# Branch hints, split first experts and three reordered places in a four-layer model with two mixtures of experts

## The chip, the cores and the metric

The kernel runs on one core of one Trainium2 chip. It is one launch that computes a whole model of four layers. The metric is the device time of one execution in microseconds (us). Before the change it is 2608.06 us, the median of three runs (2607.92 to 2608.73).

## The reference

The input `x` has 32 sequences of 64 tokens with 512 features: 2048 tokens, which the kernel takes as 16 tiles of 128. Each layer adds a residual. What is computed, cut to what matters (all in float32, and the weights are inputs):

```python
x = x + ffn0(einsum('bct,bcd->bdt', x, W0[subject]))   # attention, then shared expert
                                                       # + 7 experts, top 2 of sigmoid
x = x + ffn1(einsum('bct,bcd->bdt', x, W1[subject]))   # 32 experts, top 4, softmax gates
x = x + ffn2(x @ W.T + lora(x, adapter))               # soft mixture of 16 experts
x = x + ffn3(paged_attention(x, cache, tables, lens))  # linear layer on int8 values

# ffn1, for one token t and its 4 chosen experts:
gate = min(t @ w_gate[e] + b_gate[e], 7);  up = clip(t @ w_up[e] + b_up[e], -7, 7)
y += softmax(top4)[k] * (((up + 1) * gate * sigmoid(1.702 * gate)) @ w_down[e] + b_down[e])

# ffn2, with x_ln the layer norm of a token (gamma, beta) and x_n its l2 norm:
logits = x_n @ mu_n                                    # 16 experts x 128 slots
slots  = x_ln.T @ softmax(logits, over experts)
out    = softmax(logits, over all slots) @ (gelu(slots @ W1 + b1) @ W2 + b2)
```

`ffn0` and `ffn1` are sparse: a token goes to two or four experts only.

## The kernel before, in words

`program` (L2700) runs four functions, one for each layer; each hands its loads for the next one on, so that work of the next layer fills gaps of this one. Engines are called by name: PE is the tensor engine, DVE the vector engine, ACT the scalar engine, POOL GpSimd, SP the queue that issues most DMAs. Each engine executes its own instructions in order. A scheduler places the instructions of the program on the engines; what goes through `pin` (L314), or through an engine taken from `held`, stays in the order in which the program issues it, and `follow` in `Moe.run` chains the matmuls of the expert stage in order.

**The sparse layers.** Class `Moe` (L844; `Ranked`, L1285, for layer 1) gives each expert room for a fixed number of rows: 7 times 640 in layer 0 (35 tiles of rows), and 256 to 352 for each of 32 experts in layer 1 (71 tiles). A routing stage decides for each token its experts and its slot in them. `Moe.run` (L1142) then walks over *units*: an expert of 640 rows is two units of 320 (`UNIT`), a smaller one is one unit (L886 to L892). `turn` (L1166) transposes a gathered tile of 128 rows, in whose columns are the rows of one or more units (`of_unit`); in layer 0 DVE multiplies them by the norm's weights on the way out of PSUM (L1177), in layer 1 ACT and DVE copy in turn. `into` (L1181) does the first two matrix products of a unit, each half of 128 hidden columns in two groups of eight 128x128 matmuls `gu`, and the activation (`l0_expert`, `l1_expert`). `out_of` (L1197) multiplies one tile of rows with the last matrix, adds the bias in layer 1 and stores the tile to `ys`. Transposes of the next unit's tiles and finished tiles are woven between the groups of a unit. `rows_to` issues the gathers on POOL, `weights` and `bias_of` issue loads on SP, and `rank` is a generator that, in layer 1, sorts the experts by their load while the first unit is under way. Before the loop, all tiles of unit 0 are gathered and turned.

After the last tile, `beyond` (L1037) counts the token-expert pairs that found no room: it sums them on DVE (`more`, L1041), converts them (`number`, L1043), loads the number into a register of each engine and, under `tc.If(n > 0)` (L1048), runs a slow body for them. With these inputs the number is 0, and each engine jumps over the body. The body has several hundred instructions on DVE (some 450 in layer 0 and 880 in layer 1), and on POOL 49 and 283.

**The routing of layer 1.** `Mixed.run` (L1575) goes in steps `s` over the 16 token tiles: mix with the subject's matrix (`mix`), transpose (`turn`), logits (`route`, `logits`), pick (`choose`). From step 11 on the logits come straight as `rp` in `route`. At the steps of `GROUPS`, a generator `Ranked.put` is started for 4 or 2 tiles: alternately DVE and PE, it forms one-hot rows, counts (`at`), places and a `table` of tokens, and `go(engine)` advances those that wait for that engine. The last lines empty the generators, and `Ranked.end` (L1360) turns the table into the first experts' token lists (`tokens`, `fixedp`, `fixed`) that the first gathers wait for. The gates' softmax stands behind it in `layer1` (L1660 to L1668).

**Layer 2.** `layer2` (L1729) first sums the experts' rows for tiles 0 and 1 (`combined`, L1256: a gather `yk` by POOL and a multiply-add on DVE, L1264, four times a tile), runs `Lora` (L1878: transposes L1888, adapter product `ap` L1897, `am` on DVE L1901, product `yp` L1909 and L1910) for both tiles and the norm (`l2_norm_pieces`, L1925) of tile 0, whose multiplies with gamma and beta lie on POOL (L1937, L1938). `transpose4` (L366, matmuls at L371) turns the normed tile. Then each step `i` makes the two softmaxes of tile `i` (`Softmaxes`) and mixes tile `i-1` (`Mix`): `turn` (`ep`), `dispatch` (`hp`, `h`), `combine` (`gp`, `gT`) and `project` (`out`). Step 1 has an order of its own, written out under `early`. There `over_slots` (L2014) makes a matmul `bp` in PSUM and four subtractions and exponentials from it (`lT`, L2020), and `Mix.total` (L2080) makes the matmul `dp` (L2083) and its reciprocal `rd` (L2085). `ep`, `bp` and `dp` use the same two PSUM buffers (tag `tp`) in turn.

## Time and profile before

| | us |
|---|---|
| median of the runs | 2608.06 |
| the profiled execution | 2563.57 |
| its span | 2561.5 |
| PE busy in the span | 2442.1 |
| DVE, POOL and ACT busy | 1405.8, 905.8 and 718.3 |
| mean clock granted to PE, share of full speed | 0.974 |

The stages by time in the profiled execution, with PE's busy time and the granted clock in each:

| stretch, us | what runs there | PE busy, us | clock |
|---|---|---|---|
| 340 to 376 | end of layer 0's attention | 29.0 of 36 | 0.76 |
| 376 to 384 | start of layer 0's experts | 2.8 of 8 | 0.79 |
| 640 to 700 | end of layer 1's routing | 48.0 of 60 | 0.76 |
| 700 to 1120 | layer 1's experts | 412 of 420 | 0.98 |
| 1120 to 1160 | end of layer 1, start of layer 2 | 17.2 of 40 | 0.73 |
| 1160 to 2145 | layer 2 | 977.6 of 985 | 0.99 |
| 2290 to 2562 | layer 3's last part | 261 of 272 | |

All times and rows come from one execution, taken by the hardware profiler. A row of the timeline gives the start, the length, the engine, the line in the kernel, the operation with its output and inputs and their shapes, and in brackets how long the engine was idle before, and what ended that. `x4` is a run of like instructions. DVEq, SPq or POOLq is the part of an engine that issues. PEclk in the page is the granted clock in 40 equal slices of the span, in tenths. The profiled execution is shorter than the median of the runs by 44.5 us; differences are read against it, and its rows are not those of the median run.

### The profile page before, as it was taken

What the parts mean: (1) busy time and instruction counts of PE and PEld (TensorE: products, weight loads), DVE (VectorE), ACT (ScalarE), POOL (GpSimd) and SP (SyncE); (2) the same over time, 40 slices, a digit from 0 to 9 for tenths busy, and PEclk for the clock granted to TensorE, in tenths of its full rate; (3) what the DMA queues carried; (4) which work ended last, traced back from release to release, by engine and by line L of the source; (5) the groups of instructions that cost most, each with busy time, mean ns of one, the idle gap of its engine ahead of it and who ended that gap; (6) DMA issues with size and microseconds to landing.
All of it is one profiled execution on the core that took longest, in us unless ns stands there. A gap on an engine that the chain in (4) does not pass through costs nothing.

```text
span 2561.5 us, 42341 instructions
## 1 busy us (share of the span) xinstructions
PE 2442.1 (95%) x16533; PEld 1612.1 (63%) x16533; DVE 1405.8 (55%) x3456; ACT 718.3 (28%) x1508; POOL 905.8 (35%) x961
## 2 busy tenths in 40 slices
PE   6999989999799999979999999999999999979998
PEld 4776766666566666747666666666666665445554
DVE  3666756834745554436544544444545432657886
ACT  2444521112211111102222222222222221246664
POOL 2223325615144444523333333333333322564440
PEclk9999989999799999989999999999999999989999
DMA  2234325536456976834222222222222314424441
GB/s 102 93 138 153 128 75 199 169 120 225 161 194 229 373 275 233 296 123 150 69 73 75 74 73 73 73 76 76 74 76 76 97 57 144 165 58 134 140 140 38
DMA packets 132566, 339.35 MB, mean 132 GB/s; under 512 B 23993, under 2 KB 25049, under 8 KB 125056
## 3 DMA queue, kind: packets, MB, share of 16 engines
q1 hardware_dynamic: 90720, 188.84, 21.4%
q0 software_dynamic: 41056, 141.89, 17.6%
q10 hardware_dynamic: 576, 5.77, 0.6%
q8 instruction: 134, 2.20, 0.4%
q14 instruction: 80, 0.66, 0.1%
HBM read 245.23 MB, written 107.22 MB: 138 GB/s over the span
## 4 chain that ended last, share of the span: by engine, by line
PE 50%; DVE 3%; POOL 1%; issue 1%; DMA 1%; ACT 0%; POOLq 0%; ACTq 0%; DVEq 0%; SPq 0%
PE out L2107 9%; PE lp L1964 9%; PE zp L2041 7%; PE pp L2421 3%; PE hp L2073 3%; PE gp L2096 3%; PE y L2669 2%; PE yp L1909 2%; PE op L2647 2%; PE pT L2622 2%; PE sp L2600 2%; PE ep L2050 1%; PE kp L2573 1%; PE ap L1897 1%; PE csum L2060 1%
## 5 line engine op out<-in xcount | busy, mean ns | idle before, releaser
L1190 PE MATMUL gu<-xT,wt 128*128 128x320 f32 (+3 forms) x1472 | 396.2, 416 | 1.0 <-DVE xT L1177 0.5
L1190 PEld LDWEIGHTS gu<-xT,wt 128*128 128x128 f32 x1472 | 276.0, 191 | 120.4 <-issue 51.2
L1964 PEld LDWEIGHTS lp<-xnT,sb_mu 128*128 128x128 f32 x2048 | 236.2, 194 | 9.1 <-issue 6.7
L1964 PE MATMUL lp<-xnT,sb_mu 128*128 128x128 f32 x2048 | 239.1, 277 | 1.8 <-DVE xnT L332 1.2
L2107 PE MATMUL out<-sb_w,gT 128*128 128x512 f32 x512 | 234.2, 600 | 0.0
L2041 PE MATMUL zp<-sb_w,xnT 128*128 128x512 f32 x512 | 226.5, 592 | 0.0
L1202 PE MATMUL y<-wt,hT 128*128 128x512 f32 (+2 forms) x544 | 199.9, 595 | 1.4 <-DVE yo L1210 0.9
L360 POOL DMA_INDIRECT kvst<-kv,gidx x96 | 96.4, 1004 | 286.9 <-DMA oldkv<-kvst 205.0
L2100 DVE COPY gT<-gp 128x512 f32<-128x512 f32 x64 | 44.3, 692 | 237.9 <-PE gp L2096 237.5
L2041 PEld LDWEIGHTS zp<-sb_w,xnT 128*128 128x128 f32 x512 | 93.7, 190 | 104.8 <-issue 102.5
L2107 PEld LDWEIGHTS out<-sb_w,gT 128*128 128x128 f32 x512 | 93.6, 191 | 103.9 <-issue 95.6
L360 POOL DMA_INDIRECT kvt<-newkv,oidx x96 | 100.3, 1045 | 128.4 <-DMA kvt<-oldkv 59.2
L360 POOL DMA_INDIRECT yk<-ys,slot x96 | 97.7, 1017 | 117.1 <-DVE pre L1291 74.9
L2078 ACT ACTIVATE h<-hp 128x512 f32<-128x512 f32 x128 | 69.5, 594 | 210.5 <-PE hp L2073 210.4
L1202 PEld LDWEIGHTS y<-wt,hT 128*128 128x128 f32 (+2 forms) x544 | 72.8, 166 | 63.8 <-issue 49.1
L360 POOL DMA_INDIRECT xr<-rows,stok x101 | 97.9, 969 | 42.2 <-issue 18.5
L840 POOL TENSOR_TENSOR ga<-ga,sg 128x288 f32<-128x288 f32 (+3 forms) x64 | 50.4, 788 | 166.9 <-ACT sg L836 166.7
L2118 POOL TENSOR_TENSOR xt<-xt,bc_bias 128x512 f32<-128x512 f32 x16 | 20.6, 1288 | 211.0 <-DMA x<-xt 196.3
L2096 PEld LDWEIGHTS gp<-lT,h 128*64 128x64 f32 x2048 | 65.8, 139 | 38.8 <-issue 26.5
L2611 ACT ACTIVATE s<-s,m 128x336 f32<-128x336 f32 x128 | 72.8, 570 | 57.3 <-DVE m L2607 56.1
L1969 DVE TENSOR_TENSOR lT<-lp,cmu 128x512 f32<-128x512 f32 x64 | 43.5, 680 | 80.2 <-PE lp L1964 80.2
L2052 ACT COPY ew<-ep 128x512 f32<-128x512 f32 x64 | 37.6, 589 | 177.0 <-PE ep L2050 177.0
(456 smaller groups left out, 4641.3 us busy)
## 6 DMA issues: line engine op xcount, KB each, us to landing
ys<-yo SPq DMA_DIRECT2D x106, 256.0 KB, 3.8
oldkv<-kvst SPq DMA_DIRECT2D x96, 224.0 KB, 2.2
kvt<-oldkv SPq DMA_DIRECT2D x96, 224.0 KB, 3.3
ys<-zero SPq DMA_DIRECT2D x10, 2048.0 KB, 8.0
xt<-x SPq DMA_DIRECT2D x62, 256.0 KB, 6.0
x<-xt SPq DMA_DIRECT2D x48, 256.0 KB, 2.0
wt<-w_e SPq DMA_DIRECT2D x7, 1536.0 KB, 6.7
sb_w<-w SPq DMA_DIRECT2D x5, 1024.0 KB, 14.7
```

The lines of the kernel that those rows point to most:

```text
L360: ins = self.nc.gpsimd.indirect_dma_start(out=out, out_offset=None, in_=src, in_offset=bass.IndirectOffsetOnAxis(ap=idx, axis=0), **kw)
L1190: follow(nc.tensor.matmul(o, wj[:, c, ic * P : (ic + 1) * P], xTs[u][:, c, 0:n], start=c == 0, stop=c == 3))
L1202: follow(nc.tensor.matmul(y[row : row + n, :], hTs[e][:, ic, col : col + n], wd[:, ic, :], start=ic == 0, stop=ic == 1,))
L1909: g.first(c, nc.tensor.matmul(yp, self.xT[:, c, :], w["w_2"][:, c, :], start=c == 0, stop=False))
L1964: g.first(e + c, nc.tensor.matmul(lp[:, e, :], w["mu"][:, c, (4 * q + e) * P : (4 * q + e + 1) * P], self.xnT[:, c, :], start=c == 0, stop ...
L2041: g.first(c, nc.tensor.matmul(zp, self.xnT[:, c, :], w["w1"][:, c, cols], start=c == 0, stop=c == 3))
L2073: g.first(e + b, nc.tensor.matmul(hp[:, b, e, :], self.ews[q][r, e, :], self.z[q][r, e * P : (e + 1) * P], start=True, stop=True))
L2078: g.pin(nc.scalar.activation(self.hs[q][b], hp[:, b], AF.Gelu))
L2096: g.first(e + b + k, nc.tensor.matmul(gp[r, e, cols], self.hs[q][b][:, e, r], self.lT[q][:, e, cols], start=True, stop=True))
L2107: g.first(e, nc.tensor.matmul(self.out, self.gTs[q][:, e, :], w["w2"][:, 4 * q + e, :], start=q + e == 0, stop=q + e == 6 and q == 3))
L2421: nc.tensor.matmul(pp, xT[i][:, c, :], (w["w_kv3"] if z else wq)[:, c, :], start=c == 0, stop=c == 3)
L2611: nc.scalar.activation(p, p, AF.Exp, bias=m, scale=-1.0, accum_out=tot)
```

## The change

It does five things. The first parts of the diff are a helper and its call: `hint` puts one instruction on PE, DVE, ACT and POOL that names the branch `beyond{E}` as likely taken, three row tiles ahead of the end of `Moe.run`; the branch gets a label. The first expert's first 320 rows, in both layers, become two units of 128 and 192 rows, and the steps of the unit loop at which gathers, loads and the ranking are issued move accordingly (in layer 1 the ranking advances at three named places and not at every group). In the routing, from step 11 on the youngest generator's PE part is issued ahead of the logits and the transpose; at the end the generators are emptied in a fixed order, and the gates' softmax, now a generator in `Ranked`, is cut in two: subtraction and exponential before the last table matmuls, sum, reciprocal and product behind `end`. In layer 2, tile 0's norm is taken in pieces between the parts of tile 1's `Lora`, its gamma and beta products go to DVE, and in step 1 `total` comes ahead of `over_slots`.

```diff
--- before.py
+++ after.py
@@ -31,6 +31,7 @@
 E1, K1, V1 = 32, 4, 56
 UNIT = 320
 WB = 4
+FIRST = 128
 
 
 RANK1 = [0, 1, 3, 4, 2, 6, 5] + list(range(7, 32))
@@ -310,6 +311,17 @@
                 )
 
         return step
+
+    def hint(self, label):
+
+        traced = self.nc.cur_bb.bb.instructions
+        before = len(traced)
+        kinds = mybir.EngineType
+        self.tc.mark_branch_hint_location(
+            label, "LikelyTaken", (kinds.PE, kinds.DVE, kinds.Activation, kinds.Pool)
+        )
+        for ins in list(traced)[before:]:
+            self.pin(SimpleNamespace(ins=ins))
 
     def pin(self, ins):
 
@@ -827,12 +839,12 @@
     nc.vector.tensor_tensor(hT, up, sg, ALU.mult)
 
 
-def l1_expert(g, sb, hT, gate, up, bias):
+def l1_expert(g, sb, hT, gate, up, bias, **kw):
 
     nc = g.nc
     ga = sb.tile([P, gate.shape[1]], F32, name="ga")
     nc.vector.tensor_scalar(ga, gate, bias[:, 0:1], 7.0, ALU.add, ALU.min)
-    sg = sb.tile([P, gate.shape[1]], F32, name="sg", **(dict(bufs=2) if gate.shape[1] > P else {}))
+    sg = sb.tile([P, gate.shape[1]], F32, name="sg", **kw)
     nc.scalar.activation(sg, ga, AF.Sigmoid, scale=1.702)
     up_ = sb.tile([P, gate.shape[1]], F32, name="up")
     nc.vector.tensor_scalar(up_, up, bias[:, 1:2], 7.0, ALU.add, ALU.min)
@@ -876,7 +888,8 @@
         self.units = []
         for e, cap in enumerate(caps):
             n = cap if cap < 2 * UNIT else UNIT
-            self.units += [(e, at, n) for at in range(0, cap, n)]
+            sizes = ([] if e else [FIRST, n - FIRST]) + [n] * (cap // n - (not e))
+            self.units += [(e, sum(sizes[:k]), size) for k, size in enumerate(sizes)]
         self.ends = [sum(n for _, _, n in self.units[: u + 1]) for u in range(len(self.units))]
         self.of_unit, self.of_expert = [[] for _ in range(self.tiles)], [[] for _ in range(self.tiles)]
         for parts, sizes, whole in (
@@ -1045,7 +1058,7 @@
             number[0:1, 0:1], min_val=0, max_val=N * K,
             skip_runtime_bounds_check_because="the number of pairs is at most N * K",
         )
-        with tc.If(n > 0), ExitStack() as ctx:
+        with tc.If(n > 0, label=f"beyond{E}"), ExitStack() as ctx:
             sb = ctx.enter_context(tc.tile_pool(name=f"vs{E}", bufs=1))
             ps = ctx.enter_context(tc.tile_pool(name=f"vps{E}", bufs=2, space=PSUM))
             iota = g.c("iota")
@@ -1143,7 +1156,6 @@
 
         g, nc, tc, E, K = self.g, self.g.nc, self.g.tc, self.E, self.K
         ends, most = self.ends, max(n for _, _, n in self.units)
-        single = len(self.units) == E
         last_of = {}
         for t, parts in enumerate(self.of_expert):
             for e, *_ in parts:
@@ -1182,7 +1194,7 @@
                 e, at, n = self.units[u]
                 wg, wu, _, bias = self.parts(self.weights(e))
                 if e not in hTs:
-                    hTs[e] = sb.tile([P, 2, max(self.caps)], F32, name="hT", bufs=3 if single else 2)
+                    hTs[e] = sb.tile([P, 2, max(self.caps)], F32, name="hT", bufs=3 if self.ranked else 2)
                 gu = []
                 for wj in (wg, wu):
                     o = ps.tile([P, most], F32, name="gu", tag="gu", bufs=4)[:, 0:n]
@@ -1192,9 +1204,12 @@
                         ))
                     gu.append(o)
                     yield
-                self.act(g, sb, hTs[e][:, ic, at : at + n], *gu, None if bias is None else bias[:, ic::2])
+                kw = dict(bias=None) if bias is None else dict(bias=bias[:, ic::2], bufs=2)
+                self.act(g, sb, hTs[e][:, ic, at : at + n], *gu, **kw)
 
             def out_of(t):
+                if t == self.tiles - 3:
+                    g.hint(f"beyond{E}")
                 y = ps.tile([P, D], F32, name="y", tag="y")
                 for ic in range(2):
                     for e, col, row, n in self.pieces[t]:
@@ -1226,26 +1241,27 @@
             for u in range(len(self.units)):
                 k = 0
                 e = self.units[u][0]
-                if not (self.ranked and u == 0):
-                    self.rows_to(tiles_to(u + 2))
+                if not (self.ranked and u < 2):
+                    self.rows_to(tiles_to(max(u, 1) + 2))
                 self.bias_of(e)
-                if 1 <= u < WB - 1:
-                    self.weights(u + 1 + self.ranked, not self.ranked)
+                if 2 <= u < WB:
+                    self.weights(u + self.ranked, not self.ranked)
                 for ic in range(2):
                     for _ in into(u, ic):
                         if turned < tiles_to(u + 1):
                             turn(turned)
                             turned += 1
                         k += 1
-                        next(ranking, None)
+                        if (u, k) in ((0, 3), (1, 1), (1, 2)):
+                            next(ranking, None)
                         if k > 1 and u and (done + 1) * P <= ends[u - 1]:
                             out_of(done)
                             done += 1
                             for old in range(E):
                                 if last_of[old] == done - 1 - self.ranked:
                                     self.weights(old + WB)
-                    if self.ranked and u == 0 and ic == 0:
-                        self.rows_to(tiles_to(2))
+                    if self.ranked and u == 1 and ic == 0:
+                        self.rows_to(tiles_to(3))
                         self.weights(FIXED1)
             while done < self.tiles:
                 out_of(done)
@@ -1357,6 +1373,18 @@
                     stop=i + j == NT - 1 and k == K - 1,
                 )
 
+    def softmax(self):
+
+        nc, gates, vals = self.g.held, self.gates, self.vals
+        shape = [P, NT, K1]
+        nc.vector.tensor_tensor(gates, vals[:, :, 0:K1], vals[:, :, 0:1].to_broadcast(shape), ALU.subtract)
+        nc.scalar.activation(gates, gates, AF.Exp)
+        yield
+        tot = self.keep.tile([P, NT], F32, name="tot1")
+        nc.vector.tensor_reduce(tot, gates, AX.X, ALU.add)
+        nc.vector.reciprocal(tot, tot)
+        nc.vector.tensor_tensor(gates, gates, tot.unsqueeze(2).to_broadcast(shape), ALU.mult)
+
     def end(self, ps):
 
         g, nc, tok, ident = self.g, self.g.held, self.tok, self.g.ident
@@ -1592,8 +1620,8 @@
                     self.late.append(late)
             del pieces[:n]
 
-        def go(engine):
-            for put in list(puts):
+        def go(engine, among=None):
+            for put in list(puts if among is None else among):
                 if put[1] == engine:
                     put[1] = next(put[0], None)
                     if put[1] is None:
@@ -1608,6 +1636,8 @@
             bridge.rest(self.wp, todo[0] + 2 + s)
             if s < NT:
                 self.mix(s)
+            if s not in SPLIT:
+                go("tensor", puts[-1:])
             self.adds(s + 1)
             fill()
             if s:
@@ -1630,11 +1660,14 @@
                 go("vector")
             if s in (10, 12):
                 m.weights((s - 10) // 2)
-        while puts:
-            go("tensor")
-            go("vector")
-        assert not pieces
+        for engine in ("tensor", "vector", "vector"):
+            go(engine)
+        gates = m.softmax()
+        next(gates)
+        go("tensor")
+        assert not puts and not pieces
         m.end(self.ps)
+        next(gates, None)
 
 
 def layer1(g, bridge, combined, beside, w2):
@@ -1656,16 +1689,6 @@
         for k in ("first", "pool"):
             w2[k] = w2[k]()
         m.ready(ctx)
-
-        gates, vals = m.gates, m.vals
-        nc.vector.tensor_tensor(
-            gates, vals[:, :, 0:K1], vals[:, :, 0:1].to_broadcast([P, NT, K1]), ALU.subtract
-        )
-        nc.scalar.activation(gates, gates, AF.Exp)
-        tot = keep.tile([P, NT], F32, name="tot1")
-        nc.vector.tensor_reduce(tot, gates, AX.X, ALU.add)
-        nc.vector.reciprocal(tot, tot)
-        nc.vector.tensor_tensor(gates, gates, tot.unsqueeze(2).to_broadcast([P, NT, K1]), ALU.mult)
 
         def ahead(sb, ps, i):
             if i < NT and i % 4 == 3:
@@ -1740,14 +1763,20 @@
         x = [combined(sb, 0, 3), combined(sb, 1, 3)]
         for k in ("gamma", "beta"):
             w[k] = g.load_bcast(wp, k)
-        yp = [Lora(g, w, sb, s2, ps, x[i], i).run() for i in range(2)]
-        xn = l2_norm(g, w, sb, s2, yp[0])
+        norm = l2_norm_pieces(g, w, sb, s2, Lora(g, w, sb, s2, ps, x[0], 0).run(), nc.vector)
+        lora = Lora(g, w, sb, s2, ps, x[1], 1)
+        lora.turn()
+        next(norm)
+        next(norm)
+        lora.adapter()
+        xn = next(norm)
+        yp = lora.product()
         w["b1"] = g.load_bcast(wp, "b1", eng=nc.scalar, later=True)
         for k in ("w2", "b2"):
             w[k] = g.load(wp, k, nc.scalar, True)
         w["bias3"] = g.load_bcast(wp, "bias3", eng=nc.scalar, later=True)
         xnT, nn = g.transpose4(ps, s2, xn[0], "xnT2"), xn[1]
-        xn = l2_norm(g, w, sb, s2, yp[1])
+        xn = l2_norm(g, w, sb, s2, yp)
 
 
         last = None
@@ -1788,9 +1817,9 @@
                 mix.dispatch(0)
                 norm = l2_norm_pieces(g, w, sb, s2, lora.product())
                 next(norm)
+                mix.total()
                 soft.over_slots()
                 mix.turn(2)
-                mix.total()
                 mix.combine(0)
                 mix.dispatch(1)
             else:
@@ -1922,7 +1951,7 @@
     return out
 
 
-def l2_norm_pieces(g, w, sb, s2, yp):
+def l2_norm_pieces(g, w, sb, s2, yp, eng=None):
     nc = g.nc
     st = s2.tile([P, 6], F32, name="st")
     g.pin(nc.vector.bn_stats(st, yp))
@@ -1934,8 +1963,10 @@
     yield
     xl = sb.tile([P, D], F32, name="xl")
     g.pin(nc.vector.tensor_scalar(xl, yp, mv[:, 0:1], rs, ALU.subtract, ALU.mult))
-    nc.gpsimd.tensor_tensor(xl, xl, w["gamma"], ALU.mult)
-    nc.gpsimd.tensor_tensor(xl, xl, w["beta"], ALU.add)
+    for k, op in (("gamma", ALU.mult), ("beta", ALU.add)):
+        ins = (eng or nc.gpsimd).tensor_tensor(xl, xl, w[k], op)
+        if eng:
+            g.pin(ins)
     sq = sb.tile([P, D], F32, name="sq2", tag="mx")
     ss = s2.tile([P, 1], F32, name="ss2")
     nc.scalar.activation(sq, xl, AF.Square, accum_out=ss)
```

## Prediction

> **What bounds the kernel now.** The page's head first: engine shares, slices, granted clock.

> ```profile
> span 2561.5 us, 42341 instructions
> PE 2442.1 (95%) x16533; PEld 1612.1 (63%) x16533; DVE 1405.8 (55%) x3456; ACT 718.3 (28%) x1508; POOL 905.8 (35%) x961
> PE   6999989999799999979999999999999999979998
> PEclk9999989999799999989999999999999999989999
> ```

> TensorE (PE) is busy 95% of the span; only 119 us are idle. The slices drop at the start, near 690 us (slice 11) and near 1130 us (slice 18), and the clock drops with them. A mended stall so pays twice: its own length, and the half-clock matmuls after it. Second view: the waits of PE between 1100 and 1260 us (total, times, longest), which carry the largest holes.

> ```profile
> PE tp L1888 <- DVE xt L1264: 16.9, 1, 16.9
> PE tp L371 <- DVE xl L1947: 3.8, 1, 3.8
> PE dp L2083 <- DVE lT L2020: 3.0, 1, 3.0
> ```

> Third: the timeline across both overflow branches (L1048: `n` is 0 here, so the body is jumped over), first the end of layer 1, then of layer 0 (start, length; in brackets the idle time before and what ended it).

> ```profile
> 1122.33 0.15 DVE L1043 CAST number<-more 128x1 int32<-128x1 f32 x1
> 1124.57 1.04 SPq L289 DMA_DIRECT2D xt<-x  x2
> 1127.01 0.33 SPq L289 DMA_DIRECT2D bc_gamma<-gamma  x1
> 1129.23 0.98 POOL L360 DMA_INDIRECT yk<-ys,slot  x1 [13.63 <-DMA bc_gamma<-gamma]
> 1138.41 0.87 PE L1888 MATMUL tp<-sb_cst,xt 128*128 128x128 f32 x3 [16.94 <-DVE xt L1264]
> ```

> ```profile
> 594.46 0.15 DVE L1043 CAST number<-more 128x1 int32<-128x1 f32 x1
> 599.11 0.09 DVE L1291 MEMSET pre<- 128x32 f32 x1 [4.50 <-DVEq L1048]
> 599.15 1.02 PE L242 MATMUL gu<-hnT,sb_w_sh 128*128 128x128 f32 x7 [0.98 <-DVEq L1048]
> ```

> `number` is ready at 1122.48 and at 594.61; nothing on VectorE (DVE), PE or GpSimd (POOL) restarts until about 4.5 us later. In that gap the DMA view between 1123.0 and 1124.6 shows instruction fetches:

> ```profile
> q14 instruction: 4, 0.03, 7.1%
> q8 instruction: 1, 0.02, 4.3%
> ```

> Fourth: the starts of the experts. PE waits 5.1 us for layer 0's first row gathers (three waits) and 4.5 us for layer 1's, and then runs its first eight matmuls of 320 columns at half clock, shown by the first and second such group of layer 0:

> ```profile
> 383.61 4.34 PE L1190 MATMUL gu<-xT,wt 128*128 128x320 f32 x8 [0.52 <-DVE xT L1177]
> 388.23 2.32 PE L1190 MATMUL gu<-xT,wt 128*128 128x320 f32 x8
> ```

> **The change, part by part.** All sums are against the profiled execution: 2563.57 us, of which the span is 2561.5.

> *Hint at the end of layer 1.* A hint goes to PE, DVE, ScalarE (ACT) and POOL three row tiles, some 4 us, ahead of the branch. The chain now: CAST 1122.48, DVE/ACT/PE resumed by 1127.01 (SP's gamma load waits for DVE and ACT), POOL's first gather 1129.23, then gathers of 1.25 us each, adds, PE at 1138.41. Gathers, adds and transposes all follow POOL in order, so what POOL gains PE gains. SP, which gets no hint, resumed at 1124.57, 2.1 us after the CAST, with its wait for the last `ys` stores; I read about 2 us as the branch itself and 2.4 to 2.5 us as the fetch. POOL has 2.2 us more after the others. Bounds: 0 if the hint fetches nothing, 4.5 if POOL's own part goes too. Value 3.0, nearest to the fetch rows plus some of POOL's part. Below nothing: four hint instructions, some 0.1 us each (the small DVE rows), behind PE's own work, so no.
> [...] By the rows the sum is −3.0[...]. [...]

> *Hint at the end of layer 0.* There PE was idle only 0.98 us ahead of its first `gu`, since the shared expert's matmuls and ACT's copy (end 598.80) fill the gap; 2.05 us more are lost later, for `xt` at 605. After it: PE held by ACT until 598.80 (−0.3), gathers up to 2 us sooner. Value −0.5, bounds 0 and −1.5.

> *First expert in 128 and 192 rows.* The first unit then needs one gathered tile, not three. It adds one group of eight matmuls per weight half: 320 columns take 2.19 us per eight warm, 128 take 0.91, 192 about 1.32 (between), so four groups cost 4 × 0.04 = 0.17 us more per layer. Layer 0: the tiles' transposes stand at 378.06, 380.16, 382.01; the first `gu` could start near 379.5 and not 383.61. But DVE works in order: behind the first tile's `xT` come layer 3's length steps, whose `kfc` waited for a load until 386.14, so `xT` of tile 2 comes near 386.4 and the second unit near 386.9, where half of the head start is given back; the tile after that stands behind `qs` (landed 392.94). Half-clock work moves into waiting time. Value −0.7, bounds −3 and +1. Layer 1: transposes at 707.19, 708.66, 710.17, `gu` at 711.82; with one tile it starts near 708.9, on matmuls that run cold anyway, and the second unit's tiles come meanwhile: −1.25, bounds −2.5 and 0. The bias load moved behind the first `ys` on SP's queue, and two weight loads moved by one unit, are due tens of us later (tile 2's `yo` near 735): nothing; if that cover goes, one load of 3.8 us.

> *End of the routing.* In steps 11, 13 and 15 the pending table or `at` matmuls go ahead of the logits' transposes, and DVE's chain for tiles 12 and 13 starts about 2 us sooner, so the last logits no longer stand behind it (`lg` at 694.12, about 0.4 sooner). In the tail, four gate operations lie on DVE between the last matmuls (0.20 at 694.75, 0.21, 0.24, 0.23): their exposed issue time, some 0.55 us, moves behind the token matmuls; PE waits there 1.47, 1.25 and 3.22 us. In exchange the table of step 11 delays `rp` by 0.7, in a stage that still has other work. Value −0.8, bounds −2 and +0.7.

> *Layer 2's first norm.* Now: BatchNorm on DVE at 1150.69 behind `am` (1150.48), though `yp` was done at 1148.1; then gamma and beta on POOL, 1.26 each plus hand-overs (1153.42 to 1156.02), then square, `nn`, `xl` until 1158.37; PE waits 3.79. After: norm ahead of the second `am`, −2.1; multiplies on DVE of 0.69 and 0.65 (rows of its 128x512 operations) in place of 2.6, −1.2. `am` then comes near 1153.0, needed at 1153.71: hidden by 0.7. −3.3; bounds −2.5 (if `am` slips behind) and −3.5 (PE's wait is all there is).

> *Layer 2's step 1.* `dp` waits 3.02 us for a PSUM slot that four `lT` subtractions (1217.98 to 1220.45) give back; behind it PE runs `gp` in 1.98 against 1.15 later, `hp` 2.08 against 1.16, `ep` 1.11 against 0.60, `out` 4.24 against 3.70: 2.8 us of half clock. With the total first, `ep` waits about 1 us for `rd` (DVE, near 1218.3), `gp` starts near 1218.9, not 1221.08 (−2.2), and half of the rest comes back: −4.0. Late next: `gT`, behind the subtractions on DVE until 1220.9, and `h`, near 1224.4 ahead of its use near 1225.5. Bounds −2.5 and −5.

> Sum: 3.0 + 0.5 + 0.7 + 1.25 + 0.8 + 3.3 + 4.0 = 13.55 us, so 2563.57 becomes 2550.0. After each place PE is busy 98 to 99% (729 to 1118, 1160 to 2145), with no change in those stages' order, so gains are not swallowed. The median, 2608.06, is 44.5 above the profiled execution; nothing in the trace says where, and I carry the difference over: 2594.5.

> **Rivals.**
> *A, the hints fetch nothing* (the part doesn't do what it says[...]): the sum loses 3.5; median 2598.0. [...] 20%.
> *B, the new orders wait elsewhere:* DVE in order holds the second unit's `xT` in layer 0 (+1 in place of −0.7), routing costs 0.7, layer 1's start gives nothing, `h` holds step 1 at −2.5: 1.7 + 1.5 + 1.25 + 1.5 = 6 less; 2600.5. For: the loads at 386.14 and 392.94. 13%.
> *C, slower:* the granted clock. Its mean is 0.974, PE is busy 2442 us, so each 0.001 costs about 2.5 us. A fuller PE may be granted less: from a mean of 0.9685 on, the 13.5 us are gone; at 0.966 the time is 2594.5 + 20 = 2614.5. For: long busy stages are at 0.98 to 0.99, not 1. Against: the drops to 0.5 to 0.8 stand at idle places, which this change shortens. 5%.

> **How the numbers follow.** The likeliest case, all parts within their bounds, 62%: 2588 to 2598, 2594.5 the sum. A and B 33%, C 5%. A measurement of this kernel can tell 0.2%, 5.2 us, from no change. Faster: the likeliest case, A, and most of B, 0.88; same: B with A, 0.07; slower: C, 0.05. The range 2588 to 2602 holds the first three but for the ends.

> **What would show it.** Hint: first gather under 4.5 us after `number` at the end of layer 1, and PE's wait of 16.94 near 14; unchanged, A holds. Starts: first `gu` near 379.5 and about 3 us sooner in layer 1; a wait on `xT` at the second unit shows B. Norm: `tp` L371 waits under 1 us. Step 1: `dp`'s 3.02 gone, `gp` and `hp` near 1.15 each. A mean clock under 0.969 shows C. Wrong would be a fetch stall in the last three tiles, or a wait of the same length elsewhere.

## The result and the profile after

The changed kernel takes 2598.3 us, median of 7 runs, against 2608.73 for the kernel before: ratio 0.9954, 95% interval 0.994 to 0.9969. The forecast was 2594.5 (ratio 0.9948), range 2588 to 2602. The direction and the size held; one term of the sum, the hints, did not, and another, the routing, was too small.

The kernel before takes near 2610 us in some sessions (the first runs, the profile after, e9 to e12) and near 2563 in others (the profile before, e1 to e8), so ratios below are taken within a session and stages only between profiles of one kind. The four sessions of the experiments ran on four chips, e1 to e4 and e5 to e8 on two with the shorter times, e9 and e10 and then e11 and e12 on two with the longer.

The head of the page of the profile after:

```profile
span 2596.5 us, 42488 instructions
PE 2447.1 (94%) x16582; PEld 1617.0 (62%) x16597; DVE 1411.3 (54%) x3470; ACT 718.1 (28%) x1512; POOL 904.0 (35%) x961
PE   6999979998799999979999999999999999979998
PEclk9999989998889999989999999999999999989999
```

The span is 35 us longer than that of before although the kernel is faster; only a profile of the shorter kind, e5 below (span 2550.4), may be laid beside it. PE's waits between 1100 and 1260 us after the change (total, times, longest):

```profile
PE tp L1917 <- DVE xt L1280: 15.9, 1, 15.9
PE bp L2049 <- DVE dg L2043: 2.2, 1, 2.2
PE ep L2081 <- DVE rd L2116: 0.9, 1, 0.9
```

The waits of the first norm's transpose (3.8) and of `dp` (3.0) are gone; `ep` waits the 1 us that was foreseen; `bp` of step 0 waits 2.2 us for DVE, which was not. The first line has hardly moved: 15.9 against 16.9. The timeline across both branches shows why (start, length, idle before):

```profile
1139.37 0.15 DVE L1056 CAST number<-more 128x1 int32<-128x1 f32 x1
...
1144.30 0.33 SPq L290 DMA_DIRECT2D bc_gamma<-gamma  x1
...
1146.04 0.98 POOL L372 DMA_INDIRECT yk<-ys,slot  x1 [13.41 <-DMA xt<-x]
```

```profile
595.14 0.15 DVE L1056 CAST number<-more 128x1 int32<-128x1 f32 x1
599.37 0.09 DVE L1307 MEMSET pre<- 128x32 f32 x1 [4.08 <-DVEq L1061]
```

At the end of layer 1 it is 6.52 us from the end of `number` to the first gather (6.75 before), at the end of layer 0 4.08 us to DVE's first work (4.50 before). The stall that the hints were to take away is still there.

### The profile page after: what moved, and what is told of

The parts are those of the page before. It is cut to its first block, busy times and chain, and to the rows that moved or that the text cites. A ratio compares the mean times of both kernels' runs of the same rounds, so it can differ in the third digit from the quotient of the medians.

```text
span 2596.5 us, 42488 instructions
## 1 busy us (share of the span) xinstructions
PE 2447.1 (94%) x16582; PEld 1617.0 (62%) x16597; DVE 1411.3 (54%) x3470; ACT 718.1 (28%) x1512; POOL 904.0 (35%) x961
## 4 chain that ended last, share of the span: by engine, by line
PE 43%; DVE 10%; issue 2%; POOL 1%; DMA 0%; ACT 0%; another core or an unknown queue 0%; POOLq 0%; ACTq 0%; SPq 0%; DVEq 0%
PE out L2138 9%; PE lp L1995 7%; PE gp L2127 3%; PE pp L2452 3%; PE zp L2072 3%; PE yp L1938 2%; PE y L2700 2%; PE hp L2104 2%; PE op L2678 2%; PE sp L2631 2%; PE pT L2653 2%; DVE xt L1295 1%; PE ep L2081 1%; DVE inv L2031 1%; PE kp L2604 1%
## 5 line engine op out<-in xcount | busy, mean ns | idle before, releaser
L1202 PE MATMUL gu<-xT,wt 128*128 128x320 f32 (+5 forms) x1536 | 397.7, 406 | 4.6 <-DVE xT L1189 3.6
L1202 PEld LDWEIGHTS gu<-xT,wt 128*128 128x128 f32 x1536 | 283.6, 193 | 118.9 <-issue 49.1
L1217 PEld LDWEIGHTS y<-wt,hT 128*128 128x128 f32 (+2 forms) x544 | 73.3, 167 | 65.6 <-issue 52.4
L852 POOL TENSOR_TENSOR ga<-ga,sg 128x288 f32<-128x288 f32 (+5 forms) x66 | 50.8, 770 | 173.6 <-ACT sg L848 171.6
L2149 POOL TENSOR_TENSOR xt<-xt,bc_bias 128x512 f32<-128x512 f32 x16 | 20.2, 1264 | 220.5 <-DMA x<-xt 208.4
L2033 POOL TENSOR_TENSOR eT<-eT,inv 128x512 f32<-128x512 f32 x64 | 71.8, 1123 | 54.3 <-DVE inv L2032 46.2
L2024 ACT ACTIVATE eT<-eT 128x512 f32<-128x512 f32 x64 | 40.3, 630 | 173.9 <-DVE eT L2021 154.2
```

The source lines that it names most:

```text
L1202: follow(nc.tensor.matmul(o, wj[:, c, ic * P : (ic + 1) * P], xTs[u][:, c, 0:n], start=c == 0, stop=c == 3))
L1217: follow(nc.tensor.matmul(y[row : row + n, :], hTs[e][:, ic, col : col + n], wd[:, ic, :], start=ic == 0, stop=ic == 1,))
L2033: g.pin(nc.gpsimd.tensor_tensor(e3, e3, inv.unsqueeze(2).to_broadcast([P, 8, T]), ALU.mult))
```

## The experiments

Stages in us, read from each profile: the experts of layer 0 (first gather to `number`), routing (to `fixed`), the experts of layer 1 (to the second `number`), from there to PE's first transpose and to `bp` of step 0, then `bp` of step 1 to step 2, and of step 2 to step 15.

| | experts 0 | routing | experts 1 | first tp | bp 0 | step 1 | steps 2-15 |
|---|---|---|---|---|---|---|---|
| before | 220.0 | 109.0 | 418.9 | 15.9 | 65.0 | 56.7 | 802 |
| e1 before again | 219.9 | 111.0 | 422.6 | 15.8 | 63.8 | 56.3 | 801 |
| e2 no hints | 219.6 | 105.9 | 416.0 | 15.3 | 60.2 | 51.5 | 803 |
| e3 hints only | 219.6 | 109.3 | 421.9 | 15.6 | 64.0 | 55.2 | 802 |
| e4 layer 2 only | 219.8 | 107.6 | 422.0 | 16.0 | 60.0 | 51.6 | 804 |
| e5 changed again | 219.5 | 107.4 | 417.1 | 15.4 | 60.5 | 51.5 | 803 |
| e6 split only | 220.1 | 107.6 | 417.9 | 15.7 | 64.9 | 53.6 | 802 |
| e7 routing only | 220.2 | 103.6 | 417.5 | 15.6 | 64.3 | 55.2 | 802 |
| e8 short body | 220.0 | 105.6 | 417.3 | 11.5 | 60.2 | 56.2 | 803 |
| after (2598 us) | 220.9 | 122.9 | 421.3 | 15.0 | 58.7 | 52.5 | 827 |
| e9 early hints | 223.3 | 123.5 | 419.9 | 13.6 | 58.3 | 52.5 | 827 |
| e10 one split | 219.7 | 120.8 | 420.6 | 14.9 | 58.5 | 52.5 | 828 |
| e11 hint at 24 | 220.5 | 121.7 | 416.8 | 14.2 | 59.2 | 52.7 | 828 |
| e12 and loads | 220.9 | 119.5 | 419.1 | 11.7 | 57.0 | 52.5 | 827 |

The last five are of the longer kind. The same code scatters by 2 us in routing and 4 us in layer 1's experts (first two rows), so small gains there are taken from the timed ratios.

**e1, the kernel before once more.** No edit.

> The kernel before, unchanged, for a second profile. The first profiled execution is 44.5 us shorter than the median. Theory P (layer 2 has two rhythms): the new profile lies near 2608 us and its steps of layer 2, from bp of step 2 to bp of step 15, take about 64 us each as in the profile after (before: 61.7), with a wait of DVE's third lT subtraction behind POOL's eT product in each step; some 25 to 30 us of the 44.5 lie there. Theory S (stalls of all engines at changing places, some marked remote): the steps stay near 61.7 and the excess sits in a few gaps of 2 to 8 us elsewhere. Ratio 1.000 by both.

2564.76 us, ratio 1.0003 (0.9993 to 1.0013); profile and timed runs agree, and the steps are 61.6 us. So the 44.5 us of the forecast's sum lie between sessions and not between profiled and timed runs; theory P missed this profile. The profiles of the longer kind show what each theory named: steps of 63.6 us (25 us over 13 steps), and routing 12 to 16 us longer than in e5.

**e2, without hints.**

```diff
-                if t == self.tiles - 3:
-                    g.hint(f"beyond{E}")
```

> The changed kernel without the two hints. The prediction gave them 3.5 us. Theory N (they fetch nothing that counts: in the profile after, the first DVE work follows number by 4.1 us at layer 0's end, 4.5 before, and POOL's first gather by 6.5 at layer 1's end, 6.75 before): the time stays within 1.5 us of the changed kernel's 2598, ratio near 0.9955. Theory D ([...] the stalls of 2 to 5 us seen 17 us behind the branch at the end of layer 0 come from that): 8 to 12 us faster than the changed kernel, ratio 0.991 to 0.993, and the stretch from number of layer 0 to the cast of fixed is near 108 us, not 123. The prediction's own theory: 3.5 us slower, ratio 0.997.

2551.29 us, ratio 0.9951 (0.9936 to 0.9966): as with hints (e5). Theory N holds, and theory D, stalls that come from the hints, falls.

**e3, hints alone.** The edit of the change, on the kernel before.

> The kernel before with the two hints alone. Theory N: within 1.5 us of before, ratio 0.9995 to 1.0005, number to first gather at the end of layer 1 near 6.5. Theory D: slower by 8 to 12 us, ratio 1.003 to 1.005, with stalls of several us behind layer 0's branch. The prediction's theory: 3.5 us faster, ratio 0.9987, number to first gather near 3.7.

2563.05 us, ratio 1.0001 (0.9992 to 1.001). `number` to first gather 7.10. They neither help nor harm.

**e4, layer 2 alone.** The change's edits to `layer2` and `l2_norm_pieces`.

> The kernel before with the two edits in layer 2 alone. The prediction's theory: 3.3 + 4.0 = 7.3 us faster, ratio 0.9972, with the wait of the first norm's transpose under 1 us and bp of step 1 to bp of step 2 near 52.5 us (56.7 before). Rival (the gain is lost in layer 2's later steps, whose rhythm depends on how POOL and DVE meet): ratio 0.999 to 1.002 although both places show their gain.

2554.48 us, ratio 0.9967 (0.9954 to 0.9979): 8.5 us (5.4 to 11.8). Step 1's rows run at full clock, behind the one short wait (granted clock of the step 1.00):

```profile
1212.58 0.63 PE L2058 MATMUL ep<-sb_cst,eT 128*128 128x128 f32 x4 [0.94 <-DVE rd L2093]
1213.14 1.15 PE L2104 MATMUL gp<-lT,h 128*64 128x64 f32 x32
1214.22 1.16 PE L2081 MATMUL hp<-z,ew 64*128 64x128 f32 x16
```

Step 1 is 51.5 to 51.6 us in all three shorter profiles of the new order. With the old order, and the same wait of 3.02 us in each, it is 56.2 to 56.7 (before, e1, e8), 55.2 (e3, e7) and 53.6 (e6), at a granted clock of 0.94, 0.97 and 1.00. So 2.1 us of the gain come with the wait, and up to 3 more hang on whether the clock falls behind it, which it does not do each time.

**e5, the changed kernel once more**, in a session of the shorter kind.

> The changed kernel, unchanged, on a chip on which the kernel before takes near 2563 us. With hints that do nothing it lies within 1.5 us of the changed kernel without them (2551.3 there, ratio 0.995), with layer 2's steps at 61.7 to 61.8 us and no stalls of 2 to 5 us behind layer 0's branch: then those of the first profile after belong to the chip it ran on. [...]

2552.0 us, ratio 0.995 (0.9933 to 0.9967), routing 107.4, steps of 61.8. Harm from the hints would have shown as a ratio of 0.998 or more and a routing of over 115. The 15 us more of routing in the profile after belong to its session (e9 to e12 have them too).

Where the hints and what follows the branch stand in time, from the views of two lines (number of instructions, shortest, median and longest in ns, start of the first and of the last):

```profile
L2761 POOLq BRANCH_PREFETCH_HINT  x2: 38/46/53, 519.4 to 1105.5; - x2
L2761 DVEq BRANCH_PREFETCH_HINT  x2: 44/48/51, 579.9 to 1107.1; - x2
L1061 POOLq INC_SWDGE_SEM  x2: 863/1360/1856, 595.2 to 1123.1; - x2
```

`number` ends at 593.75 and 1118.30, so DVE's hints ran 13.8 and 11.2 us ahead of it, POOL's 74 and 12.8, and not some 4. What each engine does first behind the branch tells which of them stands there. In layer 1 the first instruction after the branch comes 3.5 to 4.2 us behind it on DVE, ACT and POOL, in e5 as in every run whose hints are absent or late (bar e8). In layer 0 it comes 2.8 to 3.9 us behind it on DVE, but 0.4 us on ACT and POOL: those two have no such stall there. POOL's first gather waits behind an instruction `INC_SWDGE_SEM` of 1.86 us at the branch's line, which stands in every run but e8; what it does no run shows.

**e6, the split alone.**

```diff
-            n = cap if cap < 2 * UNIT else UNIT
-            self.units += [(e, at, n) for at in range(0, cap, n)]
+            sizes = ([] if e else [FIRST, n - FIRST]) + [n] * (cap // n - (not e))
```

> The kernel before with the first experts' 128 + 192 rows alone (and the ranking and loads moved with them). The prediction: -0.7 in layer 0 and -1.25 in layer 1, ratio 0.9992. Rival V (second unit waits for xT behind layer 3's length steps): layer 0's stretch from the first gather to number is unchanged within 0.3 us although the first gu starts 3.5 us sooner. Rival W (layer 1 gains more than its start, since the changed kernel without hints spent 416.0 us from the cast of fixed to number, and kernels with the old start 421.9 to 422.6): layer 1 gains 5 to 6 us, ratio 0.998.

2559.91 us, ratio 0.9993 (0.9983 to 1.0003): 1.8 us, the predicted 1.95, though the interval holds 0 too. Rival V is seen in layer 0 (timeline):

```profile
378.30 1.16 PE L1191 MATMUL gu<-xT,wt 128*128 128x128 f32 x8 [0.78 <-DVE xT L1178]
...
384.43 0.17 DVE L356 CAST fh_kvlen<-ih_kvlen 128x16 f32<-128x16 int32 x1 [3.73 <-DMA ih_kvlen<-kvlen]
...
385.62 2.10 PE L1191 MATMUL gu<-xT,wt 128*128 128x192 f32 x8 [2.60 <-DVE xT L1178]
```

The first `gu` starts 4.88 us behind the first gather (8.2 to 9.0 in the shorter profiles with the old start), then DVE, which here runs its rows in the order of the program, stands 3.73 us for layer 3's length, with `xT` of the third tile behind it, and PE stands 2.60. The stretch is 220.1: all given back.

**e7, the routing order alone.** The change's edits to `Mixed.run`, `Ranked` and `layer1`.

> The kernel before with the new order of layer 1's routing end alone. The prediction: -0.8 us, ratio 0.9997, the stretch from number of layer 0 to the cast of fixed 0.8 under that of before. Kernels with the old order spent 107.6 to 111.0 us there, the changed kernel without hints 105.9: if the order itself is worth 3 us, the stretch is near 106 again, ratio 0.999.

2558.22 us, ratio 0.9985 (0.9975 to 0.9994): 3.8 us (1.5 to 6.4), not 0.8. PE's waits there hardly shrink; what changes is the clock: in the stage's last part (from 45 us behind `number` to `fixed`) PE stands idle 13.6 us in e1 and 13.3 in e7, but is busy 52.4 and 45.3. Two logits products in e1, then in e7:

```profile
671.52 1.92 PE L242 MATMUL rp<-sb_w_r,cT 128*128 128x32 f32 x8 [0.73 <-ACT cT L242]
...
684.13 1.92 PE L242 MATMUL rp<-sb_w_r,cT 128*128 128x32 f32 x8 [0.73 <-ACT cT L242]
```

```profile
673.29 1.08 PE L242 MATMUL rp<-sb_w_r,cT 128*128 128x32 f32 x8 [0.73 <-ACT cT L242]
...
681.45 1.08 PE L242 MATMUL rp<-sb_w_r,cT 128*128 128x32 f32 x8 [0.73 <-ACT cT L242]
```

The granted clock of that part is 0.71 to 0.75 in the profiles with the old order and 0.86 here; but 0.75 and 0.76 in e5 and e2, which have the new order too. One profile does not show that the order brings the clock. The timed runs point the same way: the mean clock of e7's 22 runs is 0.9764, that of the 55 of the kernel before 0.9746. Over those 55, 0.001 of clock goes with 1.7 us, so that some 3 of the 3.8 us would lie there, an estimate. It is no proof: e6's 22 runs, with the old order, have 0.9761.

**e8, overflow bodies cut to one memset.** It leaves out the slow path, which these inputs don't enter; count and branch stay.

> The kernel before with both overflow bodies cut to one small memset: the slow path that is not executed with these inputs is left out, the count, the register loads and the branch stay. It shows what a hint could give at most. If the fetch of the target page is what holds the engines: number to the first DVE work at layer 0's end falls from 4.4 to under 2 us, number to the first gather at layer 1's end from 6.7 to 2.5 to 3.5, no instruction packets about 1.5 us behind number, and the time falls by 4 to 6 us, ratio 0.998. If the engines are held by the branch itself or by the waits at the block's end: times and ratio as before, 1.000.

2554.26 us, ratio 0.9971 (0.9961 to 0.998): 7.4 us. DVE restarts 1.05 us behind `number` in layer 0, POOL 2.61 in layer 1:

```profile
1117.91 0.15 DVE L1043 CAST number<-more 128x1 int32<-128x1 f32 x1
1120.67 0.98 POOL L360 DMA_INDIRECT yk<-ys,slot  x1 [9.50 <-DMA ys<-yo]
...
1129.60 1.09 PE L1808 MATMUL tp<-sb_cst,xt 128*128 128x128 f32 x4 [12.54 <-DVE xt L1184]
```

So 7.4 us is what both branches over a full body cost. Not all of it is the stall behind the branch: with the body `INC_SWDGE_SEM` goes too, 1.86 us on POOL in layer 0 and 0.85 in layer 1. What the hints left standing is real.

**e9, hints earlier.** PE's hint stays; the others go 20 row tiles ahead in layer 0 and 45 in layer 1.

```diff
+                if t == self.tiles - AHEAD[E]:
+                    g.hint(f"beyond{E}", (kinds.DVE, kinds.Activation, kinds.Pool))
                 if t == self.tiles - 3:
-                    g.hint(f"beyond{E}")
+                    g.hint(f"beyond{E}", (kinds.PE,))
```

> The changed kernel with the hints of DVE, ACT and POOL moved ahead: 20 row tiles before the end in layer 0, 45 in layer 1[...] (DVE: 152 and 355 instructions ahead, ACT 63 and 136, POOL 58 and 204). PE's hint stays where it is. Theory C [...]: first DVE work 1 to 2.5 us behind number at layer 0's end, not 3.9 to 4.4, first gather at layer 1's end near 2.6 and not 6.9, time 3 to 7 us under the changed kernel, ratio 0.992 to 0.994. Theory L [...]: all as in the changed kernel, ratio 0.995[...].

2599.04 us against 2612.15, ratio 0.9941 (0.9921 to 0.9962); the interval holds the changed kernel's ratio. The stall is gone for DVE in layer 0 (4.08 us before, 1.43 now) and for POOL in layer 1 (first gather 3.35 behind `number`, 6.52 before):

```profile
595.90 0.15 DVE L1054 CAST number<-more 128x1 int32<-128x1 f32 x1
597.48 0.09 DVE L1308 MEMSET pre<- 128x32 f32 x1 [1.42 <-DVEq L1059]
```

The first instruction behind the branch now comes 0.4 to 0.5 us after it on every one of these engines, so the times are those of theory C, by which an earlier hint is served, and not of L. POOL's first gather in layer 0 stays at 4.45, where POOL had no stall behind the branch (0.4 us in e5). Of the 3.2 us won in layer 1 PE's transpose gets 1.4 here, 0.1 in e10 and 0.8 in e11.

**e10, layer 0's first expert whole again**, over e9.

> The same with layer 0's first expert whole again (units of 320), only layer 1's split. The split of layer 0 moved its stretch from the first gather to number by 0 to 0.3 us, so the time should stay within 1 us of the kernel with both splits, ratio equal within 0.0005; the prediction's -0.7 would make it 0.7 us slower; a gain in a later stage that hangs on it would show as more than 2 us.

2600.15 us, ratio 0.9955 (0.9939 to 0.9972): no difference that can be told from e9. Layer 0's split is worth nothing measurable.

**e11, layer 0's early hint at 24 tiles.** `AHEAD` 24 in place of 20.

> The changed kernel with early hints as before, but in layer 0 24 row tiles ahead and not 20[...]; layer 1's stay at 45. Theory C [...]: POOL's first gather at layer 0's end 1.8 to 2.5 us behind number and not 4.45, PE's wait for mm shorter by 1 to 2 us, and the rest as with 20 tiles (first DVE work 1.4, layer 1's first gather 3.35 us behind number). Time 1 to 2 us under that kernel, ratio 0.992 to 0.9945. Theory that POOL's start there hangs on something else (SP's loads, a register load): 4.45 stays, ratio as with 20 tiles.

2598.44 us, ratio 0.9952 (0.9933 to 0.9971); POOL's first gather in layer 0 stays at 4.45: the earlier hint does not move it, and what stands ahead of it is `INC_SWDGE_SEM` (1.86 us) and the waits around it (e5). The transpose in layer 1 comes 14.2 us behind `number`, since the first rows land late:

```profile
1135.16 0.98 POOL L370 DMA_INDIRECT yk<-ys,slot  x1 [10.26 <-issue]
1135.27 0.34 SPq L291 DMA_DIRECT2D bc_gamma<-gamma  x1
...
1142.18 0.75 DVE L1281 SCALAR_TENSOR_TENSOR xt<-yk,gates,xt 128x512 f32<-128x512 f32 x1 [10.38 <-DMA yk<-ys,slot]
```

**e12, and gamma and beta loaded later.**

```diff
-        for k in ("gamma", "beta"):
-            w[k] = g.load_bcast(wp, k)
+        lora = Lora(g, w, sb, s2, ps, x[0], 0)
+        lora.turn()
+        for k in ("gamma", "beta"):
+            w[k] = g.load_bcast(wp, k, eng=nc.scalar, later=True)
```

> The same, with layer 2's gamma and beta loaded from ACT's queue behind its copy of tile 0's transposes and no longer from SP's ahead of the gathers. With early hints the first gathers left 3.2 us sooner, but their rows came 6.6 us after the first issue and not 4.4, beside the loads on SP's queue, and PE's first transpose gained only 0.1 to 1.4 us. If the two broadcasts hold the gathers back: number to PE's first transpose 11.5 to 12.5 us (13.6 to 14.9 with early hints, 15 to 15.4 without), 1 to 3 us faster than the kernel with 24 tiles. If other transfers do (the x tiles, the last ys): within 0.5 us of it. The loads land near 21 us behind number and are needed near 25: no new wait.

2592.65 us, ratio 0.9932 (0.9918 to 0.9947), the lowest ratio seen, though its interval overlaps e11's. The first rows now land 4.2 us behind their issue, not 7.0, and the transpose comes at 11.7:

```profile
1136.12 0.98 POOL L370 DMA_INDIRECT yk<-ys,slot  x1 [10.26 <-issue]
...
1140.35 0.75 DVE L1281 SCALAR_TENSOR_TENSOR xt<-yk,gates,xt 128x512 f32<-128x512 f32 x1 [7.60 <-DMA yk<-ys,slot]
...
1144.46 1.09 PE L1921 MATMUL tp<-sb_cst,xt 128*128 128x128 f32 x4 [12.71 <-DVE xt L1281]
```

## Why the prediction was right, and where it was not

In the sessions of e1 to e8 the parts alone give: hints +0.3 us, layer 2 −8.5, split −1.8, routing −3.8, together −13.8; the changed kernel −12.8 (−17 to −8). The forecast was −13.55. The total held because two terms were too small where one was wrong: that it came out within 1 us is luck.

*Hints: −3.5 forecast, 0 measured.* The step that failed is that a hint three tiles ahead is served. No row told that, and two readings behind the term were wrong. The gap was split into 2 us of branch and 2.4 to 2.5 of fetch, by SP; but on DVE and POOL the branch is over 0.4 to 0.8 us behind `number` (SP's 2.1 us were its other waits), and the stall behind it is 3.5 to 4.2 us on three engines in layer 1. And in layer 0 POOL, which was to start its gathers sooner, has none (e5).

Why the late hint is not served on DVE, ACT and POOL: not for want of time, since it ran 11 to 14 us ahead in layer 1, longer than any of these stalls. The instruction packets tell more; they go over two queues. On q8 one starts 1.2 us behind PE's hint in the profile after, 12.4 us ahead of the second `number` (12.6 in e5), where the profile before has none; and PE's two branches take 0.39 and 0.44 us, 3.44 and 3.59 in the profile before. So PE's hint is served, and q8 reads as PE's queue. On q14 the last packet in the profile after starts 39.0 us ahead of the second `number`, before the hints, and seven follow within 7 us behind it. In e9 the hints stand 45 row tiles ahead in layer 1: in the profile after the store of that tile starts 242 us ahead of `number`, with four q14 packets in between. In e12, with the same hints in layer 1, four packets follow within 7 us and not seven. The packets agree with a hint that is served at a later fetch of its engine; that it is so, and which packet holds the branch's target, is not shown. The feared harm, a stall that the hints bring, did not come (e3).

*A later term, which the prediction had only as "a wait of the same length elsewhere":* had the hint worked, its gain would have met the loads on SP's queue (e9 to e12). "What POOL gains PE gains" was wrong until these were moved: then PE's transpose came 3.3 us sooner (15.0 to 11.7), with 3.0 forecast.

*Layer 2: −7.3 forecast, −8.5 measured.* The first norm's transpose comes 32.2 us behind `number` in e5, 36.0 in the profile before: 3.8, the whole wait, with 3.3 forecast; `am` came in time. Step 1 gains 4.8 against e1 (56.3 to 51.5), 4.0 forecast: `hp`, `ep` and `out` came back to full clock wholly, not by half. Against e6, whose old order kept the clock, it gains 2.1: the forecast took the loss of clock as sure. `bp` of step 0 waits 2.0 us for DVE in the new order, and still comes 60.0 to 60.5 us behind `number`, not 63.8 to 65.0.

*Split: −1.95 forecast, −1.8 measured (not told from 0)*, but otherwise shared: layer 0 gives everything back at the place that the prediction named, layer 1's first `gu` starts 2.7 us sooner (5.5 and 8.2 behind `fixed`).

*Routing: −0.8 forecast, −3.8 measured.* The waits were counted, the clock was not, and a stage at a clock of 0.71 to 0.75 had more to win from the clock than from its waits. The prediction said so of the whole kernel at the start and then left it out of this term. That the new order is what raised the clock is not shown (e7).

*Rivals.* A, hints that gain nothing, was what happened, with the other terms making up for it; its 20% was the author's estimate. Its ratio would be 0.9961, the forecast's 0.9948; the interval of the measurement, 0.994 to 0.9969, holds both, so the time alone does not choose, and the experiments do. B's mechanism in layer 0 is real, the rest of it did not come. C did not: the mean clock rose, from 0.974 in the profile before to 0.977 in e5.

## What to carry to other kernels

## What the runs showed of the hardware that was not expected

One kernel, the one before, takes 1.7 to 1.9% longer in some sessions than in others (2562 to 2563 and 2609 to 2612 us), at mean clocks of 0.974 to 0.975 and 0.972, and most of the difference sits in two places. The first is layer 2's steady steps, where PE's waits for DVE in steps 2 to 15 add up to 20.8 us in the profile after and to 0.9 in the one before. There two engines meet. In the profile before DVE's third `lT` of a step starts 0.02 us ahead of POOL's `eT`, in the profile after it starts 1.1 us behind it. Its idle time in steps 2 to 14 is 0.4 us in the shorter profiles and 1.5 to 1.8 in every one of the longer.

```profile
1445.08 0.69 DVE L1969 TENSOR_TENSOR lT<-lp,cmu 128x512 f32<-128x512 f32 x1 [0.44 <-PE lp L1964]
1445.10 1.05 POOL L2002 TENSOR_TENSOR eT<-eT,inv 128x512 f32<-128x512 f32 x1
```

```profile
1456.93 1.05 POOL L2033 TENSOR_TENSOR eT<-eT,inv 128x512 f32<-128x512 f32 x1
1458.06 0.69 DVE L2000 TENSOR_TENSOR lT<-lp,cmu 128x512 f32<-128x512 f32 x1 [1.57 <-PE lp L1995]
```

In the longer kind `lT` starts within 0.25 us of the end of `eT`, as if POOL held DVE up. But what the profile names is PE's `lp`, whose signal comes 1.1 us behind its last matmul, and in steps 1 and 15 of both kinds `eT` starts 0.26 to 0.29 us ahead and `lT` runs beside it. So how the 1.1 us arise is open. The second place is the routing: in the longer kind ACT, DVE and PE have gaps of 2 to 10 us some 20 to 30 us behind the first branch, with hints early or late. Why is open too.
